# Winograd convolutions: the first output tile of each image takes its products in another order

## The chip, the cores and the metric

The kernel runs on one core of one Trainium2 chip. The metric is the device time of one execution in microseconds. Three runs of the kernel before took 3323.92, 3324.4 and 3329.04 us; the median is 3324.4 us.

## What is computed

The reference is a small image network on three images of 256 channels and 48 x 48 points, in float32, of four residual layers. Layer 0 is a block with attention, layer 3 a state-space scan over the points. The change lies in layers 1 and 2, two 3 x 3 convolutions:

```python
# layer 1: each image has its own kernel, mixed from 8 experts
pooled = x.mean(axis=(2, 3))
routing = sigmoid(pooled @ routing_ws)                    # 3 images x 8 experts
ws = einsum('ne,eoihw->noihw', routing, weight)           # 3 x 256 x 256 x 3 x 3
x = x + conv3x3(gn(x), ws)                                # image n with kernel ws[n]
# layer 2: one kernel and a bias
x = x + conv3x3(gn(x), weight) + bias
```

`gn` is a group norm of 32 groups, which has no learned factors.

## The kernel before, in words

**The convolution.** It is done along image rows in the Winograd form with four outputs and six parts: each group of six neighbouring columns gives six sums (the parts), the three columns of a kernel also give six, and product i of an output tile multiplies part i of the image with part i of the kernel. `products` (L1587) makes one such product: six matmuls of 128 x 128 weights on 128 x 288 values (three kernel rows, two halves of the input channels, `ct` 0 and 1), which add up in one PSUM room `ps_c`. There are five such rooms (pool `ps1`, L1584). The profile counts each of these float32 matmuls twice, so a product is 12 records and an output tile of six products 72.

**The input side.** `input_transform` (L316) works on half an image (24 of 48 rows, `h`). ScalarE first writes the normed values into `xpad` (L331, two instructions), with one row of the other half as a halo, so that it reads x in both halves. Then twelve VectorE steps (L345 to L356) make the six parts `vt`: parts 1 and 3 from two helpers `c` and `e`, parts 4 and 5 from `c` and `e` made anew, last parts 0 and 2 (the outer ones), which use the second `c` and `e`. `xpad` has one buffer, `vt` two. The transform of the next half is made while TensorE multiplies the present one.

**The kernel side.** In the first layer `mixed` (L265) makes the kernel of the next image beside the products of the present one: for each of 8 experts six pieces `wconv` of 128 x 768 come in by DMA (pool `wst`, six buffers), and VectorE adds each, times its routing factor, into `u` (L296). One piece in six is instead added up by TensorE in two spare banks (L282) and copied into `u` by ScalarE at the end (L290). Then `kernel_transform` (L254) turns the three kernel columns, which lie in parts 0, 1 and 2 of `u`, into the six parts, with six VectorE steps for each `ct`: L259 writes part 4, L260 part 5, L262 part 3, L263 part 1. Parts 0 and 2 stay as they came. In the second layer `plain` (L302) loads one kernel for all images.

**The output side.** `output` (L1599) makes one tile: 128 output channels (`m`) of half an image (`h`). It asks for products 1 and 3, then 4 and 5; of each pair ScalarE copies the second out of PSUM (L1607) and VectorE makes the sum and the difference (L1609, L1611). Eight more VectorE steps add these into x, in place (L1616 or L1618, and L1619). At last products 0 and 2 are asked for, and VectorE adds each into x straight from PSUM (L1621, the outer sums).

**The order.** The images go 2, 1, 0, in the first layer and then in the second: six units of two halves of two tiles. The loop over them stands at L1699. For each half the transform of the next half is asked for first, then the two tiles; after each tile 13 steps of the kernel that is being mixed. `moments` (L1628) and `next_norm` (L1648) make the statistics for the next norm on ScalarE. In the second layer the first steps of the scan go in between products (`between`, L1670). The program doesn't fix the order of instructions on an engine here: a scheduler sets it at build time, by what depends on what and its own guess of the costs, and engines then work in that order. Only the part before the convolutions is held in the written order (`keep_order`); in it lies the transform of the first half of image 2 (L1090).

Of the kernel before, what the change touches and what calls it, by code (L numbers as in the profile page):

```python
# [12 lines left out]
ALU = mybir.AluOpType  # L13
# [71 lines left out]
def net(  # L85
# [230 lines left out]
    def input_transform(b, h, sc, sh):  # L316

        rows = HR + 2
        size = rows * PW
        t = pad.tile([P, 4, CT * size + 2], F32, name="xpad")  # L320

        nc.gpsimd.memset(t[:, :, 0 : CT * size + 1 : PW], 0.0)  # L322
        at = (0 if h == 0 else HR + 1) * PW
        for ct in range(CT):
            nc.gpsimd.memset(t[:, :, ct * size + at : ct * size + at + PW], 0.0)
        lo = 1 if h == 0 else 0
        first = h * HR - 1 + lo
        for ct in range(CT):
            src = xs[b][:, ct, :].rearrange("p (j r c) -> p j r c", j=4, c=TW)
            dst = t[:, :, ct * size : (ct + 1) * size].rearrange("p j (r c) -> p j r c", c=PW)  # L330
            nc.scalar.activation(  # L331
                dst[:, :, lo : lo + HR + 1, 1:], src[:, :, first : first + HR + 1, :],
                AF.Identity, bias=sh[:, ct : ct + 1], scale=sc[:, ct : ct + 1],
            )

        def column(j, at):
            return t[:, j, at : at + CT * size].rearrange("p (r c) -> p r c", c=PW)[:, :, :TW]

        d = [column(j, at) for j, at in ((3, 0), (0, 1), (1, 1), (2, 1), (3, 1), (0, 2))]
        vt = vp.tile([P, 6, CT, (HR + 2) * TW], F32, name="vt")  # L340
        o = [vt[:, i].rearrange("p t (r c) -> p (t r) c", c=TW) for i in range(6)]
        c = pad.tile([P, CT * rows, TW], F32, name="wc")
        e = pad.tile([P, CT * rows, TW], F32, name="we")
        tt, stt = nc.vector.tensor_tensor, nc.vector.scalar_tensor_tensor
        stt(c, d[2], -4.0, d[4], ALU.mult, ALU.add)  # L345
        stt(e, d[1], -4.0, d[3], ALU.mult, ALU.add)
        tt(o[1], c, e, ALU.add)
        tt(o[3], c, e, ALU.subtract)
        tt(c, d[4], d[2], ALU.subtract)
        tt(e, d[3], d[1], ALU.subtract)  # L350
        stt(o[4], e, 2.0, c, ALU.mult, ALU.add)
        stt(o[5], e, -2.0, c, ALU.mult, ALU.add)
        tt(o[0], d[0], d[2], ALU.subtract)
        stt(o[0], o[0], 4.0, c, ALU.mult, ALU.add)
        tt(o[2], d[5], d[3], ALU.subtract)
        stt(o[2], e, -4.0, o[2], ALU.mult, ALU.add)  # L356
        return vt

    def routing(b, psum, tag, stats):
# [23 lines left out]
    with ExitStack() as l0:  # L383
# [131 lines left out]
        def hidden(b, c):  # L515
            wf, fb = mlp[b]
            f = fpool.tile([P, 2, CH], F32, name="f")
            pf = pair()
            for m in range(2):
                nc.tensor.matmul(  # L520
                    pf[:, m, :CH], wf[:, m * P : (m + 1) * P], chunk(cur[b], c),
                    start=True, stop=True,
                )
            for m in range(2):
                nc.scalar.activation(f[:, m, :], pf[:, m, :CH], AF.Gelu, bias=fb[:, m : m + 1])
            return f
# [10 lines left out]
        with ExitStack() as p2:  # L537
# [4 lines left out]
            if not exact:  # L542

                sums = vpool.tile([P, 3 * NB * len(SCH) * 16], F32, name="sums")
                nc.gpsimd.memset(sums, 1.0)

            for i in range(NB):
# [399 lines left out]
                vt = vpool.tile([P, NT, 384], F32, name="vt")  # L947
# [27 lines left out]
                if i + 1 < NB:  # L975
# [4 lines left out]
                    for b in ORDER:  # L980
                        for c in range(NCH):
                            f = hidden(b, c)
# [66 lines left out]
        i = NB - 1  # L1049
# [17 lines left out]
        for n, b in enumerate(ORDER):  # L1067
            held = None
            for c in range(NCH):
                f = hidden(b, c)  # L1070
                if held is not None:
                    add_back(i, *held)
                held = b, c, f
                aside(3 if n == 2 and c % 2 else 2)
            add_back(i, *held)
            stats = [
                small.tile([P, NCH, 6], F32, name=f"xst{m}", bufs=2) for m in range(CT)
            ]
            for c in range(NCH):
                concatenated(b, c, *ahead.pop(0))  # L1080

                z = n * NCH + c + 2
                if 3 <= z < len(chunks):
                    ahead.append(parts(*chunks[z]))
                if c:
                    take_stats(b, c - 1, stats)
                if b == 0 and c == 3:
                    vp = late_pool("vp", 2, last_pools)
                    pad = late_pool("pad", stack=last_pools)
                    first_v = input_transform(2, 0, *norms[2])  # L1090
                aside(3 if n < 2 or c < 2 else 99)
            take_stats(b, NCH - 1, stats)
            if b:
                curpools[b].close()
            small_steps.append(routing(b, psm, "m", stats))
# [485 lines left out]
    with ExitStack() as l1:  # L1581
# [5 lines left out]
        def products(u, vt, m, i):  # L1587
            pc = ps.tile([P, 512], F32, tag="c", name="ps_c")
            for ct in range(CT):
                for dy in range(3):  # L1590
                    nc.tensor.matmul(  # L1591
                        pc[:, :HN], u[:, i, dy, ct, m * P : (m + 1) * P],
                        vt[:, i, ct, dy * TW : dy * TW + HN],
                        start=ct == 0 and dy == 0, stop=ct == CT - 1 and dy == 2,
                    )
            between()
            return pc[:, :HN]

        def output(b, h, m, u, vt, bias):  # L1599

            xj = xs[b][:, m, :].rearrange("p (j n) -> p j n", j=4)[:, :, h * HN : (h + 1) * HN]
            tt, stt = nc.vector.tensor_tensor, nc.vector.scalar_tensor_tensor
            sums = []
            for i, j in ((1, 3), (4, 5)):
                pa, pb = products(u, vt, m, i), products(u, vt, m, j)
                cb = tmp.tile([P, HN], F32, name="cb")
                nc.scalar.copy(cb, pb)  # L1607
                add = tmp.tile([P, HN], F32, name=f"add{i}")
                tt(add, pa, cb, ALU.add)  # L1609
                sub = tmp.tile([P, HN], F32, name=f"sub{i}")  # L1610
                tt(sub, pa, cb, ALU.subtract)  # L1611
                sums += [add, sub]
            p, q, r, s = sums
            for k, (minus, more, f) in enumerate(((p, r, 1.0), (q, s, 2.0), (p, r, 4.0), (q, s, 8.0))):
                if bias is None:
                    tt(xj[:, k], xj[:, k], minus, ALU.subtract)  # L1616
                else:
                    stt(xj[:, k], xj[:, k], bias[:, m : m + 1], minus, ALU.add, ALU.subtract)  # L1618
                stt(xj[:, k], more, f, xj[:, k], ALU.mult, ALU.add)  # L1619
            for i, k, f in ((0, 0, 1.5), (2, 3, 6.0)):  # L1620
                stt(xj[:, k], products(u, vt, m, i), f, xj[:, k], ALU.mult, ALU.add)  # L1621


        units = [(layer, b) for layer in range(2) for b in ORDER]
# [38 lines left out]
        def transformed(n):  # L1663
            k, h = halves[n]
            return input_transform(units[k][1], h, *norms[units[k][1]])
# [4 lines left out]
        def between():  # L1670
            next(pending, None)
            if at_unit >= 4:
                next(early, None)
# [23 lines left out]
        vt = first_v  # L1697
        behind, pending = None, iter(())
        for n, (k, h) in enumerate(halves):  # L1699
            layer, b = units[k]  # L1700
            at_unit = k
            if k == 3 and h == 0:
                w3_rooms()
                w3_loads()
            ahead = transformed(n + 1) if n + 1 < len(halves) else None
            u = weights[B if layer else b]
            for m in range(2):
                output(b, h, m, u, vt, v("l2_bias", 0, 2) if layer else None)
                for _ in range(13):
                    next(beside.get(k, iter(())), None)  # L1710
                if m == 0 and behind is not None:
                    store_tokens(*behind)
                    behind = None
            vt = ahead
            if layer:
                behind = b, h
            if h == 1:
                for _ in pending:
                    pass
                pending = next_norm(layer, b)  # L1720
                next(pending)
# [12 lines left out]
    with ExitStack() as l3:  # L1734
# [172 lines left out]
        k = chunks[0]  # L1907
# [7 lines left out]
        for s, (at, m, h) in enumerate(steps):  # L1915
            if m == 0 and h == 1 and at + 2 <= last:
                fetch(at + 2)
            for part in range(8):
                j = 4 * m + 2 * h + part // 4
                scan(s, part)  # L1920
                decay(8 * s + part + 3)
                if (m, h, part) in busy:
                    g, q = parts_of_step[part]
                    keep_busy(tiles[s][:, g, q, 1 : P + 1], busy[m, h, part])
                if part == 0 and h == 0:
                    c, n = (at, m + 1) if m + 1 < DI else (at + 1, 0)
# [31 lines left out]
        k = chunks[last]  # L1958
# [122 lines left out]
```

## Time and profile before

| | |
|---|---|
| median of three runs | 3324.4 us |
| the profiled execution's own time | 3327.43 us |
| its span, first to last instruction | 3325.7 us |
| TensorE busy (matmul) | 3138.1 us, 94% |
| VectorE busy | 2864.1 us, 86% |
| ScalarE busy | 2391.5 us, 72% |
| GpSimd busy | 1334.5 us, 40% |
| convolutions (L1591), first to last matmul | 1499.6 to 1998.0 us |
| matmuls of L1591 | 429.8 us busy, 409 ns mean, x1728 |
| mixing on VectorE (L296) in that stretch | 68.3 us, 1009 ns mean, x70 |

Times inside the profile count from the start of the span. Engines are PE (TensorE's matmuls), PEld (its weight loads, beside the matmuls), DVE (VectorE), ACT (ScalarE), POOL (GpSimd) and SP (which issues DMAs). A row of a timeline gives start, length, engine, line, operation and tiles, and in brackets the idle time of that engine before it and what ended it. A row with xN merges N instructions that follow each other. PEclk is the clock that TensorE was granted, 1.00 being full speed. The convolutions begin after the attention block (which ends at about 1499 us), and the scan follows them.

### The profile page before, as it was taken

How to read it: one execution, taken by the hardware profiler on the slowest of the kernel's cores; microseconds unless marked ns; L12 is line 12 of the kernel's file. 1: busy time of each engine (PE TensorE's matmuls, PEld its weight loads, DVE VectorE, ACT ScalarE, POOL GpSimd, SP SyncE). 2: the span in 40 equal slices, each digit the busy share in tenths (PEclk: the TensorE clock that was granted, in tenths of full speed). 3: DMA queues.
4: the chain of work that ended last, by engine and by line, in shares of the span. 5: the costliest groups of instructions: out<-in, count | busy, mean ns of one | idle time of the engine just before them, and what ended most of it. 6: DMA issues, size and time to landing. Idle time of an engine off the chain costs nothing.

```text
span 3325.7 us, 54145 instructions
## 1 busy us (share of the span) xinstructions
PE 3138.1 (94%) x20890; PEld 1551.0 (47%) x20890; DVE 2864.1 (86%) x3234; ACT 2391.5 (72%) x3663; POOL 1334.5 (40%) x457
## 2 busy tenths in 40 slices
PE   7999999999999999989999997999999999999985
PEld 4334343353343434546677773444444444444442
DVE  3799989968988998379985458999999999999997
ACT  2688888838888887422224457888888888888884
POOL 0000000000000000120000008999999999999997
PEclk9999999999999999999999998999999999999997
DMA  4000000010000001485611025555555555556552
GB/s 167 32 8 10 8 8 7 8 47 5 8 7 8 10 8 32 154 292 186 216 54 42 34 65 138 139 133 126 132 140 147 134 132 132 125 135 144 142 127 56
DMA packets 182158, 290.76 MB, mean 87 GB/s; under 512 B 34737, under 2 KB 148465, under 8 KB 179970
## 3 DMA queue, kind: packets, MB, share of 16 engines
q1 hardware_dynamic: 168658, 267.15, 29.9%
q10 hardware_dynamic: 13232, 20.06, 1.9%
q8 instruction: 165, 2.70, 0.4%
q14 instruction: 103, 0.84, 0.1%
HBM read 236.24 MB, written 50.64 MB: 86 GB/s over the span
## 4 chain that ended last, share of the span: by engine, by line
PE 55%; DVE 30%; ACT 8%; issue 4%; DMA 2%; POOL 0%; SPq 0%; DVEq 0%; ACTq 0%; POOLq 0%
DVE hs L1862 20%; PE ps_s L640 16%; PE acc L653 14%; PE ps_c L1591 8%; DVE hs L1810 3%; ACT ps_da L1854 2%; PE ps_s L1033 2%; PE ps_y L464 2%; PE ps_m L667 2%; PE ps_m L713 1%; DVE u L296 1%; PE acc L531 1%; PE ps_g L1224 1%; PE ps_s L520 1%; PE ps_y L1896 1%
## 5 line engine op out<-in xcount | busy, mean ns | idle before, releaser
L644 ACT ACTIVATE pt<-ps_s 128x1024 f32<-128x1024 f32 x972 | 942.3, 1022 | 154.8 <-PE ps_s L640 142.1
L1862 DVE TENSOR_TENSOR_SCAN hs<-ps_da,hs 128x385 f32<-128x385 f32 x1152 | 1001.9, 934 | 6.8 <-ACT ps_da L1854 4.9
L859 DVE TENSOR_TENSOR part<-part,pt 128x2048 f32<-128x2048 f32 x396 | 906.5, 2289 | 41.3 <-ACT pt L644 18.5
L1854 ACT ACTIVATE ps_da<-dtr,u 128x384 f32<-128x384 f32 x1152 | 651.1, 580 | 119.5 <-DVE hs L1862 108.7
L164 POOL TENSOR_TENSOR rstd<-ve,mhalf 128x2 f32<-128x2 f32 (+1 forms) x26 | 16.7, 642 | 1486.8 <-DVE ve L162 1486.8
L640 PE MATMUL ps_s<-q,kt 32*128 32x512 f32 (+1 forms) x4320 | 576.4, 592 | 0.1
L653 PE MATMUL acc<-pt,vt 128*32 128x512 f32 (+1 forms) x4320 | 521.0, 561 | 0.2
L1591 PE MATMUL ps_c<-vt,u 128*128 128x288 f32 x1728 | 429.8, 409 | 10.8 <-DVE u L263 8.4
L1879 POOL TENSOR_TENSOR hc<-hs,x 128x3072 f32<-128x3072 f32 x72 | 405.2, 5628 | 12.6 <-DVE hs L1862 8.7
L1879 POOL TENSOR_TENSOR hc<-hs,bc 128x3072 f32<-128x3072 f32 x71 | 400.3, 5638 | 9.9 <-DVE hs L1862 5.5
L1591 PEld LDWEIGHTS ps_c<-vt,u 128*128 128x128 f32 x1728 | 328.8, 191 | 106.6 <-DVE u L263 9.1
L640 PEld LDWEIGHTS ps_s<-q,kt 32*128 32x128 f32 x4320 | 195.3, 183 | 199.1 <-issue 120.2
L653 PEld LDWEIGHTS acc<-pt,vt 128*32 128x32 f32 x4320 | 94.4, 108 | 353.4 <-issue 326.7
L1896 PE MATMUL ps_y<-hc,u 128*32 128x384 f32 x2304 | 228.5, 516 | 2.9 <-POOL hc L1879 2.9
L1275 PE MATMUL ps_g<-u 128*128 128x384 f32 x576 | 195.9, 493 | 23.0 <-ACT u L1271 23.0
L1828 POOL TENSOR_TENSOR hs<-dtur,x 128x1536 f32<-128x1536 f32 x72 | 209.0, 2903 | 7.0 <-DMA dtur<-dtud 7.0
L1828 POOL TENSOR_TENSOR hs<-dtur,bc 128x1536 f32<-128x1536 f32 x72 | 209.6, 2912 | 0.0
L1275 PEld LDWEIGHTS ps_g<-u 128*128 128x128 f32 x576 | 108.7, 191 | 107.1 <-ACT u L1271 34.3
L1896 PEld LDWEIGHTS ps_y<-hc,u 128*32 128x32 f32 x2304 | 62.0, 112 | 145.4 <-issue 130.1
L1607 ACT COPY cb<-ps_c 128x288 f32<-128x288 f32 x48 | 19.1, 398 | 152.0 <-PE ps_c L1591 145.0
L322 POOL MEMSET xpad<- 128x212 f32 x12 | 5.7, 472 | 287.4 <-ACT xpad L1642 225.6
L1394 PE MATMUL ps_g<-u 128*128 128x384 f32 x288 | 106.6, 503 | 12.4 <-ACT sz L1402 7.8
(275 smaller groups left out, 4128.8 us busy)
## 6 DMA issues: line engine op xcount, KB each, us to landing
wconv<-in_we SPq DMA_DIRECT2D x144, 384.0 KB, 4.7
dtr<-dtd SPq DMA_DIRECT2D x288, 192.0 KB, 3.7
dtur<-dtud SPq DMA_DIRECT2D x288, 96.0 KB, 4.2
wconv<-xd SPq DMA_DIRECT2D x36, 384.0 KB, 3.7
x<-bcd SPq DMA_DIRECT2D x72, 192.0 KB, 4.7
dtd<-x SPq DMA_DIRECT2D x36, 384.0 KB, 3.0
dtuq<-dtud SPq DMA_DIRECT2D x288, 48.0 KB, 2.0
bc<-bcd SPq DMA_DIRECT2D x72, 192.0 KB, 4.8
```

The lines of the kernel that those rows point to most:

```text
L640: nc.tensor.matmul(s[:, j, cols], kt[r, mt * P : (mt + 1) * P], q[r, :n], start=True, stop=True,)
L644: nc.scalar.activation(p[:, h0 : h0 + 2, :], s, AF.Exp)
L653: nc.tensor.matmul(acc[h * HD : (h + 1) * HD, :n], vt[:, mt, g * P + h * HD : g * P + (h + 1) * HD], p[:, h, cols], start=mt == 0, stop=mt ...
L859: ): nc.vector.tensor_tensor(part, first, p, ALU.add)
L1275: nc.tensor.matmul(bank[m % 2], w3v["taps"][:, m, tap, :], w3v["xi"][:, m % 3, tap : tap + CH], start=tap == 0, stop=tap == DCONV - 1,)
L1394: nc.tensor.matmul(bank[j], w("in", ct * 512 + m * P, P), k.xn[:, ct, DCONV - 1 :], start=ct == 0, stop=ct == CT - 1,)
L1591: nc.tensor.matmul(pc[:, :HN], u[:, i, dy, ct, m * P : (m + 1) * P], vt[:, i, ct, dy * TW : dy * TW + HN], start=ct == 0 and dy == 0, stop ...
L1828: nc.gpsimd.tensor_tensor(states(s)[:, :, 2:4, 1:], chunks[at].rows[m][1].unsqueeze(1).broadcast_to([P, 2, 2, CH]), b_rows(s, 0, 2), ALU.mult,
L1854: nc.scalar.activation(slots[n % 3][:, 1 : CH + 1], chunks[at].rows[m][0][:, q, :], AF.Exp, scale=amat[:, col : col + 1],)
L1862: nc.vector.tensor_tensor_scan(b, slots[(8 * s + part) % 3][:, : CH + 1], b, 0.0, ALU.mult, ALU.add)
L1879: nc.gpsimd.tensor_tensor(hc, tiles[s][:, :, :, 1:], cb.broadcast_to([P, 2, 4, CH]), ALU.mult)
L1896: nc.tensor.matmul(k.y_ps[32 * q : 32 * q + 32, :CH], fold, hc[:, g, q, :], start=False, stop=h == 1 and g == 1,)
```

## The change

In the first tile of each image (h = 0, m = 0) `output` asks for the outer products 0 and 2 first and adds them into x, then for products 4 and 5, then for 1 and 3. The eight steps that add the pairs into x stay as they were, after both pairs. All other tiles keep their order. For h = 0 `input_transform` makes the parts in the order 0, 2, 4, 5, 1, 3: it makes the second `c` and `e` first, and the first `c` and `e`, which parts 1 and 3 need, last. For h = 1 it keeps its order. No instruction is added or taken away, and no size is changed.

```diff
+        def odd():
+            stt(c, d[2], -4.0, d[4], ALU.mult, ALU.add)
+            stt(e, d[1], -4.0, d[3], ALU.mult, ALU.add)
+            tt(o[1], c, e, ALU.add)
+            tt(o[3], c, e, ALU.subtract)
+
+        def outer():
+            tt(o[0], d[0], d[2], ALU.subtract)
+            stt(o[0], o[0], 4.0, c, ALU.mult, ALU.add)
+            tt(o[2], d[5], d[3], ALU.subtract)
+            stt(o[2], e, -4.0, o[2], ALU.mult, ALU.add)
+
         c = pad.tile([P, CT * rows, TW], F32, name="wc")
         e = pad.tile([P, CT * rows, TW], F32, name="we")
         tt, stt = nc.vector.tensor_tensor, nc.vector.scalar_tensor_tensor
-        stt(c, d[2], -4.0, d[4], ALU.mult, ALU.add)
-        stt(e, d[1], -4.0, d[3], ALU.mult, ALU.add)
-        tt(o[1], c, e, ALU.add)
-        tt(o[3], c, e, ALU.subtract)
+        if h:
+            odd()
         tt(c, d[4], d[2], ALU.subtract)
         tt(e, d[3], d[1], ALU.subtract)
+        if not h:
+            outer()
         stt(o[4], e, 2.0, c, ALU.mult, ALU.add)
         stt(o[5], e, -2.0, c, ALU.mult, ALU.add)
-        tt(o[0], d[0], d[2], ALU.subtract)
-        stt(o[0], o[0], 4.0, c, ALU.mult, ALU.add)
-        tt(o[2], d[5], d[3], ALU.subtract)
-        stt(o[2], e, -4.0, o[2], ALU.mult, ALU.add)
+        if h:
+            outer()
+        else:
+            odd()
...
+            def ends():
+                for i, k, f in ((0, 0, 1.5), (2, 3, 6.0)):
+                    stt(xj[:, k], products(u, vt, m, i), f, xj[:, k], ALU.mult, ALU.add)
+
+            first = h == 0 and m == 0
+            if first:
+                ends()
             sums = []
-            for i, j in ((1, 3), (4, 5)):
+            for i, j in ((4, 5), (1, 3)) if first else ((1, 3), (4, 5)):
...
-            p, q, r, s = sums
+            p, q, r, s = sums[2:] + sums[:2] if first else sums
...
-            for i, k, f in ((0, 0, 1.5), (2, 3, 6.0)):
-                stt(xj[:, k], products(u, vt, m, i), f, xj[:, k], ALU.mult, ALU.add)
+            if not first:
+                ends()
```

## The prediction

> **What bounds the kernel now.** First the page's busy rows and chain of waits: TensorE holds the convolutions (its line L1591 is 8% of the chain), VectorE the scan after them. So the question is whether TensorE stands still inside the convolutions, 1499 to 1998 us. The waits of TensorE in that stretch (columns: who waited, for whom, total us, times, longest) answer it:
>
> ```profile
> PE ps_c L1591 <- DVE u L263: 8.4, 2, 6.2
> PE ps_g L282 <- DMA wconv<-in_we: 3.4, 2, 2.2
> PE ps_c L1591 <- DVE u L262: 1.1, 1, 1.1
> ```
>
> Only the kernel transform (L262, L263) costs more than transfers do. The timeline of TensorE says where (start, length, work, idle before it):
>
> ```profile
> 1584.71 2.74 PE L282 MATMUL ps_g<-wconv,each 128*128 128x384 f32 x8
> 1588.00 0.38 PE L186 MATMUL ps_gm<-mv,gmat 128*128 128x2 f32 x2 [0.54 <-ACT xpad L1635]
> 1594.55 20.77 PE L1591 MATMUL ps_c<-vt,u 128*128 128x288 f32 x72 [6.17 <-DVE u L263]
> ...
> 1658.04 17.62 PE L1591 MATMUL ps_c<-vt,u 128*128 128x288 f32 x72
> 1675.50 2.74 PE L282 MATMUL ps_g<-wconv,each 128*128 128x384 f32 x8
> 1680.46 7.54 PE L1591 MATMUL ps_c<-vt,u 128*128 128x288 f32 x30 [2.22 <-DVE u L263]
> 1689.09 22.09 PE L1591 MATMUL ps_c<-vt,u 128*128 128x288 f32 x90 [1.09 <-DVE u L262]
> ```
>
> A tile is 36 matmuls, 72 records. The tile at 1658.04 took 17.62 us, the one after the 6.17 us wait 20.77. The table by stretches of L1591 (busy PE, PEld, then granted clock, DMA share, GB/s) says why:
>
> ```profile
> 1588.00:1591.00 3.00, 0.00 (x0) 0.00 (x0) 0.92 0.95 327
> 1591.00:1594.50 3.50, 0.00 (x0) 0.00 (x0) 0.50 0.09 36
> ...
> 1596.00:1598.00 2.00, 2.00 (x5) 1.36 (x5) 0.50 0.93 356
> ...
> 1600.00:1602.00 2.00, 2.00 (x8) 1.59 (x7) 0.82 0.96 332
> 1602.00:1606.00 4.00, 4.00 (x18) 3.11 (x18) 1.00 0.42 166
> ```
>
> The clock fell to half during the wait and stayed there until about 1601: 20.77 - 17.62 = 3.15 us more. Around the 2.22 us wait at 1680 the same table gives 1.00: no such loss.
>
> **What the Trainium skill says.** "TensorE: Matmul & The Clock Gate", Part 1: TensorE runs at half clock after an idle window of about 3.4 us and recovers after about as long of sustained work. The trace agrees in kind: 0.50 after the 6.17 us wait, 1.00 after 2.22; here the half clock lasted some 6.5 us of work. "Perfetto Trace Analysis", Sequencer Loop: an engine's instructions go into a queue, and one that is read waits there for its semaphores. The trace agrees: the products of parts 0 and 2 had their operands at 1588.8, but stood behind the part that waited until 1594.5. "Trainium Kernel Development and Optimization", Key Constraints: all queues' DMAs run on the same 16 engines; the 0.93 to 0.96 DMA share at 1596 to 1602 agrees.
>
> **The change, part by part.** No instruction is added or removed; the built order differs only within the convolutions, and SP's and POOL's orders not at all.
>
> (a) Image 1's first tile. Before: from the end of the mixing products (1584.71 + 2.74 = 1587.45) to the end of the tile (1594.55 + 20.77 = 1615.3) are 27.9 us, for 17.6 of work: 10.2 lost (idle 6.7, half clock 3.15, and the norm's small product, 0.4, which the built order puts later). After: part 0 of the kernel needs only the last mixing step, which ends before VectorE's first transform step at 1586.48. So the tile starts at 1587.45, each product 17.62 / 6 = 2.9 us. Part 2's second half is wanted at 1591.8 and is there at 1588.8 (ScalarE's L290: 1587.85 + 0.96). From VectorE's timeline: part 4 is there at 1591.9 (L259) and wanted at 1594.7; part 5 at 1593.6 (L260), wanted at 1597.6; part 1, L263, at 1594.5 and 1598.5, wanted at 1599 and 1600.6. No wait is left, so the clock stays up: -10.2 us at the end of this tile, now 1604.9. The image parts were ready (1557.6).
>
> (b) The two outer sums (L1621) now open the tile, and hold two of five PSUM rooms until VectorE adds them into x. They must also wait until ScalarE has read x for the next half (L331, 1591.57 + 2.67 = 1594.2). In the built order they stand on VectorE behind 12 kernel-transform steps and the 11th and 12th of the next half's input-transform steps: the first at 1586.48 + 12 x 0.87 + 11 x 0.72 = 1604.8, done by 1605.3, the second by 1606.4. The first product that needs the room is the next tile's, behind two mixing products (1.3): 1606.2. Cover 0.9 us: I take 0, at worst 1 to 2. Without that cover each us late is a us of TensorE.
>
> (c) Image 1's stage, in which VectorE and DMA mix image 0's kernel:
>
> ```profile
> 1594.50:1680.40 85.90, 83.69 (x322) 62.90 (x322) 79.75 (x133) 17.41 (x27) 1.38 (x4) 0.96 0.64 215
> ```
>
> (Columns: PE, PEld, DVE, ACT, POOL, clock, DMA share, GB/s.) VectorE is busy 79.75 of 85.9 us, so the lead of 10.2 can't all survive. The mixing ended before at 1671.93 (first L258). Up to there VectorE waited some 6.0 us: 4.5 for wconv transfers, 1.1 for a copy, the rest for POOL. The built order now puts 8 steps of the last tile (8 x 0.37 = 3.0) ahead of that end. If no wait shrinks: 1674.9. If all go: 1668.9. I followed TensorE, VectorE and the mixing transfers by hand through the built order (4.7 us from issue to landing, the page's median): VectorE still waits for transfers, TensorE meets four new waits for wconv of 1.6, 1.3, 0.3 and 1.1 us (in-order, all too short to lose the clock), and the mixing ends at about 1671. Its last TensorE product, whose buffer comes free just before, runs to 1672.6 in place of 1678.24. The lead is then 5.6.
>
> (d) Image 0's first tile. Before it ended at 1689.09 + 3.5 x 2.9 = 1699.3, 21.1 after 1678.24: 3.5 lost to waits (2.2 + 1.1). After: part 2 waits for L290, which stands on ScalarE behind the moments (L1635, 2.1 us) of the last tile; about 1673.6, wanted at 1676.5. Part 4 is there at 1676.4, wanted at 1677.9; part 1 at 1683.1, wanted at 1685.1. No wait: 1672.6 + 17.0 (one matmul already done) = 1689.6, so 9.7 ahead. The next tile's first product takes the room of the tile's last and waits for its copy (L1607, 0.4 and the hand-over): +0.6. Left: 9.1. (From the last mixing product to the end of the tile 17.0 us in place of 21.1, so (d) alone gives 4.1.)
>
> (e) Image 2 and the plain convolution. At 1499.67 TensorE is held by ScalarE's L1038, then by VectorE's statistics (1.14 and 0.59): both stay. Part 0 is ready by 1497.5. In the second layer TensorE waited for nothing up to 1855; there the built order puts the outer sums ahead of the transform, so that their rooms are free some 8.5 us into the image, and the earliest user comes at 14.5. 0 +- 0.5.
>
> (f) After the convolutions nothing is changed, and the scan waits for their end through the last store; the lead goes through whole.
>
> Sum: 10.2 (a) - 4.6 (c) + 4.1 - 0.6 (d) = 9.1 us; taken against the profiled execution, 3327.4 - 9.1 = 3318.3. That execution lies 3.0 above the median of the runs, 3324.4; the forecast for the median is 3315.3. Bounds from (c) and (b): mixing at 1674.9 and 1 us of (b) leave 9.1 - 3.9 - 1 = 4.2; mixing at 1668.9 gives 9.1 + 2.1 = 11.2, up to some 12.4 without the new wconv waits.
>
> **Rivals.** Lead eaten: image 1's stage is paced by mixing, and TensorE's earlier start is returned to wconv waits there. For it: VectorE 93% busy, DMA share 0.64. Against: the first-tile waits of image 0 still go. It gives 4.2 to 6.5 us: 3318 to 3320, "same" by the bound below. Mixing keeps up: the transfers, asked for earlier, land earlier, so VectorE's waits go: 3312 to 3313. Slower: the outer sums hold their rooms through the whole next input transform in every image. Price: ScalarE's moments and L331 take until 8 us into an image, the transform another 8.6; rooms are wanted at 14.5, so 2 to 3 us in each of six images, and past some 3.4 us the clock's 3.15 on top; 6 x 3 = 18 takes 9.1 to -9: 3333. It decides once the sums run later than 14.5 us after the image's first product; the built order, which puts them first in the second layer, speaks against it. That the order doesn't change after all is excluded: the built program has part 0 first at all six places.
>
> **How the numbers follow.** A difference under 0.2% (6.6 us) can't be told from no change here. Forecast (6.6 to 11 us gained) 0.62; mixing keeps up 0.13; lead eaten 0.20; slower 0.05. Hence faster 0.75, same 0.20, slower 0.05. The range runs from 3311.0 (12.4 gained, 1 for the runs' scatter) to 3320.5 (4.2 gained).
>
> **What would show it.** TensorE at 1587 without idle and clock 1.00 to 1604 (a); no L1591 wait on the outer sums of more than 1 us (b); waits of L282 for wconv of about 4 us in all, and the last mixing step at 1669 to 1675 (c); image 0's first tile ended near 1690 (d); no new waits after 1700 (e). A wait over 3.4 us anywhere in the stage, with 0.50 behind it, would make the forecast wrong.

## The result, and the profile after

The kernel after takes 3315.88 us (median of 14 runs, 3307.68 to 3322.15) against 3325.24 us before (14 runs, 3322.44 to 3329.51): 9.4 us less, ratio 0.9969 with a 95% interval of 0.996 to 0.9977. (The ratio is an estimate from all runs; that of the two medians alone would be 0.9972.) The forecast was 3315.3 us, a gain of 9.1. The profiled execution took 3316.7 us with a span of 3314.9; the one before took 3327.43, so the two profiles are 10.7 us apart.

In the new file the products stand at L1603 (L1591 before), the outer sums at L1617 (L1621), the copy at L1626 (L1607), `moments` at L1654 (L1635); L258 to L290 are unmoved. TensorE's waits inside the convolutions, without the one before their first product and some on other things of 0.6 us or less (who waited, for whom, total us, times, longest):

```profile
PE ps_g L282 <- DMA wconv<-in_we: 4.4, 4, 2.0
PE ps_gm L186 <- DVE mv L183: 3.0, 1, 3.0
PE ps_c L1603 <- ACT cb L1626: 0.4, 1, 0.4
```

The three waits on the kernel transform (L262, L263), 9.5 us in all, are gone. The timeline of TensorE at the same places, rows left out between them (start, length, work, idle before it):

```profile
1569.05 2.91 PE L282 MATMUL ps_g<-wconv,each 128*128 128x384 f32 x4 [1.96 <-DMA wconv<-in_we]
1584.74 2.74 PE L282 MATMUL ps_g<-wconv,each 128*128 128x384 f32 x8
1587.32 17.62 PE L1603 MATMUL ps_c<-vt,u 128*128 128x288 f32 x72
1669.19 1.53 PE L282 MATMUL ps_g<-wconv,each 128*128 128x384 f32 x4 [0.30 <-DMA wconv<-in_we]
1670.56 17.14 PE L1603 MATMUL ps_c<-vt,u 128*128 128x288 f32 x70
1688.18 19.18 PE L1603 MATMUL ps_c<-vt,u 128*128 128x288 f32 x78 [0.37 <-ACT cb L1626]
1984.08 3.07 PE L1603 MATMUL ps_c<-vt,u 128*128 128x288 f32 x12
```

Image 1's first tile follows the mixing products at once and takes 17.62 us where it took 20.77. Image 0's first tile, but for one matmul done earlier, begins at 1670.56 and is one unbroken row. The last matmul of the convolutions ends at 1987.15, against 1998.44 before: 11.3 us ahead. Of that 0.6 us is lost before the end of the execution. From the timeline before:

```profile
1995.37 3.07 PE L1591 MATMUL ps_c<-vt,u 128*128 128x288 f32 x12
```

The stretches of L1603 that stood at half clock before, now (length of the stretch, busy PE, PEld, then clock, DMA share, GB/s):

```profile
1591.00:1594.50 3.50, 3.50 (x16) 2.77 (x15) 1.00 0.15 61
1596.00:1598.00 2.00, 2.00 (x10) 1.53 (x9) 1.00 1.06 351
1600.00:1602.00 2.00, 2.00 (x10) 1.58 (x9) 1.00 1.02 375
```

Image 1's stage as a whole, in the same view for all engines (length, busy PE, PEld, DVE, ACT, POOL, clock, DMA share, GB/s):

```profile
1587.33:1670.57 83.24, 81.84 (x328) 61.30 (x327) 81.32 (x136) 25.71 (x42) 2.09 (x7) 1.00 0.67 230
```

All that VectorE waits for from 1587 to 1672 us (who, for whom, total us, times, longest):

```profile
DVE u L296 <- DMA wconv<-in_we: 1.5, 3, 0.9
DVE gsc L216 <- POOL rstd L164: 0.4, 1, 0.4
```

VectorE is now busy 81.32 of 83.24 us, 98%; its waits for transfers fell from 4.5 to 1.5 us. TensorE is as busy, 81.84 us, and stood still for 1.4 us only. So neither engine alone limits this stage now; both are full.

### The profile page after: what moved, and what is told of

It reads as the page before. It is cut to its first block, busy times and chain, and to the rows that moved or that the text cites. A ratio compares the mean times of both kernels' runs of the same rounds, so it can differ in the third digit from the quotient of the medians.

```text
span 3314.9 us, 54140 instructions
## 1 busy us (share of the span) xinstructions
PE 3140.8 (95%) x20890; PEld 1553.0 (47%) x20890; DVE 2865.4 (86%) x3234; ACT 2392.1 (72%) x3663; POOL 1335.4 (40%) x457
## 4 chain that ended last, share of the span: by engine, by line
PE 58%; DVE 28%; ACT 7%; issue 4%; DMA 2%; POOL 0%; SPq 0%; DVEq 0%; ACTq 0%; POOLq 0%
DVE hs L1881 20%; PE ps_s L652 16%; PE acc L665 14%; PE ps_c L1603 10%; DVE hs L1829 3%; ACT ps_da L1873 2%; PE ps_s L1045 2%; PE ps_y L476 2%; PE ps_m L679 2%; PE ps_m L725 1%; PE acc L543 1%; PE ps_g L1236 1%; PE ps_s L532 1%; DMA wconv<-in_we 1%; DVE u L296 1%
## 5 line engine op out<-in xcount | busy, mean ns | idle before, releaser
L1603 PE MATMUL ps_c<-vt,u 128*128 128x288 f32 x1728 | 430.6, 409 | 1.7 <-ACT x L1050 1.4
L1603 PEld LDWEIGHTS ps_c<-vt,u 128*128 128x128 f32 x1728 | 329.4, 191 | 98.1 <-issue 3.8
L1626 ACT COPY cb<-ps_c 128x288 f32<-128x288 f32 x48 | 19.3, 402 | 140.1 <-PE ps_c L1603 138.0
```

The lines of the kernel that those rows point to most:

```text
L1603: nc.tensor.matmul(pc[:, :HN], u[:, i, dy, ct, m * P : (m + 1) * P], vt[:, i, ct, dy * TW : dy * TW + HN], start=ct == 0 and dy == 0, stop ...
```

## The experiments

The convolutions begin anywhere from 1494.6 to 1499.8 us in the profiles of eight kernels whose code is the same up to there, and single times scatter by more than that. So beside the time two lengths are read from each trace. Stage 1 goes from the end of the last mixing product of image 1's kernel to that of image 0's; the rest from there to the end of the convolutions. Each length is of one execution: in the four profiles in which image 1's first tile kept the old order and nothing was added ahead of it, stage 1 took 89.3 to 90.8 us, so a difference of some 1.5 us between two rows says little. (The ends of rows overlap the next row by 0.15 us, which is taken off; the expectations quote 411.0 for the 411.1 here.) The times are medians; "ratio" is that to the kernel before on the same chip, whose medians were 3325.1 to 3325.4.

| kernel | time, us | ratio, 95% interval | stage 1 | the rest | sum |
|---|---|---|---|---|---|
| before | 3325.2 | | 90.8 | 320.3 | 411.1 |
| after | 3315.9 | 0.996 to 0.9977 | 83.2 | 316.6 | 399.8 |
| image 1 only | 3323.4 | 0.9986 to 1.0003 | 85.4 | 326.2 | 411.6 |
| image 0 only | 3325.3 | 0.9994 to 1.0011 | 89.3 | 321.1 | 410.5 |
| images 1 and 0 | 3316.8 | 0.9964 to 0.9985 | 83.8 | 316.8 | 400.5 |
| the other four | 3326.7 | 0.9995 to 1.0011 | 90.2 | 319.9 | 410.2 |
| products only | 3319.2 | 0.9971 to 0.9986 | 88.4 | 316.5 | 404.9 |
| kept busy | 3326.0 | 0.9994 to 1.0011 | 87.7 | 321.5 | 409.2 |
| rooms held | 3318.3 | 0.9972 to 0.9985 | 83.1 | 318.3 | 401.4 |
| later routing | 3317.7 | 0.997 to 0.9987 | 84.2 | 316.7 | 400.9 |
| image 0, norm later | 3322.9 | 0.9984 to 0.9997 | 90.2 | 318.5 | 408.7 |
| before, 4 experts | 3316.7 | 0.9966 to 0.9989 | | | 402.3 |
| image 1 only, 4 experts | 3312.1 | 0.9942 to 0.9969 | | | 395.3 |
| after, 4 experts | 3310.3 | 0.9944 to 0.9971 | | | 394.4 |

### One image at a time

Units are numbered in the order of work, so 1 is image 1 and 2 is image 0 of the first layer. `input_transform` gets its new order in the same units. In the first run NEW is (1,).

```diff
-            first = h == 0 and m == 0
+            first = h == 0 and m == 0 and at_unit in NEW
```

> The change for image 1 alone; the other five images keep the old order. Theory (mixing paces image 1's stage, and the two first tiles are worth something only together): TensorE starts image 1's first tile at 1587 without idle, 10.2 us ahead, and reaches image 0's first tile 5 to 7 us ahead. There the old order waits for part 1, which comes only some 2 us earlier, since it hangs on the end of the mixing. So the 2.2 us wait for L263 grows to 7 to 9 us, the clock falls to half, and 3.15 us go on top: the time is within 2 us of before (3323 to 3327). Rival (the gains of the two tiles add up): the 5.6 us that the forecast left of the first tile go through whole, about 3319.6.

Measured: 3323.4 us, 1.7 below before, not to be told from no change. The timeline of TensorE:

```profile
1584.57 17.62 PE L1603 MATMUL ps_c<-vt,u 128*128 128x288 f32 x72
1667.40 2.78 PE L282 MATMUL ps_g<-wconv,each 128*128 128x384 f32 x8
1678.00 33.90 PE L1603 MATMUL ps_c<-vt,u 128*128 128x288 f32 x132 [7.19 <-DVE u L263]
```

L1603 in the stretches of 4 us around its restart (length, busy PE, PEld, clock, DMA share, GB/s):

```profile
1674.00:1678.00 4.00, 0.00 (x1) 0.00 (x1) 0.54 0.55 189
1678.00:1682.00 4.00, 4.00 (x10) 2.82 (x10) 0.61 0.00 0
```

Image 1's first tile is as fast as in the kernel after, and stage 1 is 5.4 us shorter than before. Then TensorE meets the end of the mixing: it waits 7.19 us in place of 2.22 and 1.09, and works at half clock behind that. The rest grows by 5.9 us. The lead is lost whole in this trace, as the theory said.

> The change for image 0 alone. Theory: TensorE arrives at image 0's first tile at the same moment as before, and loses 0 in place of 3.5 us there, less 0.6 for the copy: 3.5 to 4.1 us below before, 3321.1 to 3321.7; no wait for L262 or L263 at that tile, the 6.2 us wait and the half clock at image 1 stay. Rival (the image 0 part is hidden by what comes after): 3325. Rival (most of the whole gain sits here): below 3319.

The same line with NEW = (2,). Measured: 3325.3 us. The gain of 3.5 us did not come, and the theory was wrong. The timeline:

```profile
1670.70 2.74 PE L282 MATMUL ps_g<-wconv,each 128*128 128x384 f32 x8
1673.28 29.26 PE L1603 MATMUL ps_c<-vt,u 128*128 128x288 f32 x120
1702.38 0.28 PE L186 MATMUL ps_gm<-mv,gmat 128*128 128x2 f32 x2
1702.52 4.13 PE L1603 MATMUL ps_c<-vt,u 128*128 128x288 f32 x16
1709.36 0.38 PE L195 MATMUL ps_gv<-gd,gmat 128*128 128x2 f32 x2 [2.71 <-DVE gd L192]
1709.60 67.90 PE L1603 MATMUL ps_c<-vt,u 128*128 128x288 f32 x272
```

The first tile has no wait, as forecast. But 36 us later TensorE stands 2.71 us before the second small product of image 1's norm, which VectorE prepares (L192, at 1709.16), and the clock fell to 0.84 and 0.73 in the two stretches of 4 us from 1708. VectorE, without idle from 1678 on, was still behind with the kernel transform and the sums of image 0, and an earlier TensorE ran into it. The row behind the wait takes 67.90 us; the same 272 records took 66.21 in the kernel before:

```profile
1715.27 66.21 PE L1591 MATMUL ps_c<-vt,u 128*128 128x288 f32 x272
```

So the wait and the slower clock cost 4.4 us, more than the 3.3 us of waits that are gone (2.22 and 1.09).

> The change for image 0 alone once more, with the two small products of image 1's norm put six products later into image 0's stage, behind more of TensorE's work. Theory (the 3.5 us won at image 0's first tile were given back to the wait of 2.7 us on VectorE's part of that norm, and to the slower clock behind it): the wait goes and the gain comes through, from the end of image 2's mixing to the end of the convolutions some 407 us, the time 3 to 4 us below before. Rival (VectorE is late itself, and the wait turns up at the next thing that needs it): 410 to 411 us, the time as before.

```diff
-            for _ in range(9):
+            for _ in range(15 if not layer and b == 1 else 9):
```

Measured: 3322.9 us, 1.0 to 5.3 us below before (from the interval), and 408.7 us in place of 410.5, between the 407 of the theory and the 410 to 411 of the rival. Part of the gain comes through. A wait of 1.47 us is left at the same product, later by 18 us (1727.25). The interval overlaps that of image 0 alone, so that the norm's product took the gain rests above all on the 4.4 us in the trace of image 0 alone; this run bears it out in part.

> The change for images 1 and 0 together; image 2 and the second layer keep the old order. Theory (each of the two is worth nothing without the other): from the end of image 2's mixing products to the end of the convolutions some 400 us as in the changed kernel (399.8), against 411.0 before, 411.6 with image 1 alone and 410.5 with image 0 alone in their profiled runs; the time 9 to 12 us below before, 3313.5 to 3316.5. Rival (the single changes add up, and the rest of the gain comes from the other images): 1.7 + 0, some 3323.5.

NEW = (1, 2). Measured: 3316.8 us and 400.5 us in the trace. The two images alone bring 1.7 and 0 us, both together 8.6; in the traces these are -0.5, 0.6 and 10.6 us. The rival, that they add up, is out.

> The change for image 2 and the three images of the second layer alone, images 1 and 0 in the old order. Theory: no wait there hangs on the order of the parts, 0 +- 1.5 us against before (3325.2). Rival (rooms held by the outer sums): up to 2 to 3 us per image, 3330 or more. Rival (image 2 pays by itself): below 3323.

NEW = (0, 3, 4, 5). Measured: 3326.7 us, ratio 0.9995 to 1.0011, and no new wait in the trace. The other four images do nothing for the time that these runs can show.

### Half of the mixing left out

Image 0's kernel is mixed from four experts in place of eight, in the kernel before, in the kernel after, and in the one with image 1 alone changed. What is left out is half of the additions on VectorE, of the transfers and of the mixing products.

```diff
-        for e in range(EXPERTS):
+        for e in range(4 if b == 0 else EXPERTS):
...
```

> The kernel before, with image 0's kernel mixed from four of the eight experts: half of the mixing that stands beside image 1's stage is left out. Its transform is then ready long before image 0's first tile. Theory: the 3.5 us of waits at image 0's first tile go, four pairs of mixing products (5.2 us) and most of the 3.4 us of wconv waits too; the 6.2 us wait and the half clock at image 1 stay: 3314 to 3317.

> The changed kernel, with image 0's kernel mixed from four of the eight experts, as in the run beside it. Theory (the mixing eats the lead of image 1's first tile): without half of the mixing the lead of 10.2 us goes through whole, 9 to 11 us below the kernel before with four experts. Rival (the lead is lost to something else, or the first tile yields no more than the 5.6 us that were left of it): 4 to 6.5 us below it.

> The change for image 1 alone, with image 0's kernel mixed from four of the eight experts (half of that mixing is left out). With all eight experts this change brought 1.7 us. Theory (there the mixing turned the lead into a wait at image 0's first tile): with half the mixing no wait is left to take it, and the lead of 8 to 10 us goes through: from the end of image 2's mixing products to the end of the convolutions 392 to 395 us, against 402.3 of the kernel before with four experts (394.4 with the whole change); the time 3306 to 3311. Rival (the first tile of image 1 yields little by itself): 400 us or more, 3314 or more.

Measured: 3316.7, 3310.3 and 3312.1 us. The difference of the first two is 6.4 us, short of the 9 to 11 of the theory and within the 4 to 6.5 of its rival; with 10 and 5 runs the two intervals overlap, and the times alone do not decide. The traces give 402.3, 394.4 and 395.3 us, so 7.9 us for the whole change and 7.0 for image 1 alone. Image 1's first tile in this run of before took 19.35 us, not 20.77, so that its wait, half clock and norm product cost 8.8 us there; the 7.9 is most of that. The timeline of image 1 only:

```profile
1587.62 17.62 PE L1603 MATMUL ps_c<-vt,u 128*128 128x288 f32 x72
1651.55 43.92 PE L1603 MATMUL ps_c<-vt,u 128*128 128x288 f32 x180 [1.42 <-DVE sub L1630]
```

Image 0's first tile stands inside the second row, without a wait, where it had waited 7.19 us with all eight experts. There image 1 alone had reached the end with nothing (-0.5 us in the trace). So it is the mixing that takes the lead. Whether its additions or its transfers set the pace these runs don't separate, since both are halved. Nor are the 7.9 and 7.0 us the lead alone: a wait for the norm later on, 1.49 us in this run of before, is 0.25 us with the whole change and none with image 1 alone.

### Single costs

> The kernel before, with the products of parts 0 and 2 made once more ahead of image 1's first tile and thrown away: TensorE works in 5.8 of the 6.7 us in which it stood. Nothing else is changed. Theory of the half clock: the tile takes 17.6 us in place of 20.8, since the clock stays at 1.00, and ends 3.15 us earlier; of that little reaches the end, since the mixing paces the stage: 3323 to 3325.5. Rival (the 3.15 us go through whole): 3322. Rival (the slow start has another cause, such as late operands): the tile still takes 20 us or more.

```diff
+            if at_unit == 1 and h == 0 and m == 0:
+                pc = ps.tile([P, 512], F32, tag="c", name="ps_w")
+                for i in (0, 2):
...
             sums = []
```

Measured: 3326.0 us, no gain. The timeline:

```profile
1597.67 17.73 PE L1591 MATMUL ps_c<-vt,u 128*128 128x288 f32 x72 [1.13 <-DVE u L263]
1681.56 30.87 PE L1591 MATMUL ps_c<-vt,u 128*128 128x288 f32 x120 [3.24 <-DVE u L263]
```

The tile takes 17.73 us: the 3 us were the half clock, and it came from standing still. Stage 1 is 3.1 us shorter than in the profile before (1.6 to 2.5 against the other profiles with the old first tile). Image 0's first tile then has one wait of 3.24 us in place of 2.22 and 1.09, and the clock falls to 0.54 behind it (1681 to 1684), so the rest is 1.2 us longer. Of the 3.1 us 1.9 are left in the trace, and none in the medians, whose interval allows a gain of up to 2 us.

> The changed kernel, but the two outer sums of each first tile are added to x only after the eight steps of the inner sums, so that they hold two of the five PSUM rooms some 4 to 5 us longer. If the rooms are as scarce as the prediction said (cover 0.9 us, beyond it each us late is a us of TensorE): waits of 3 to 4 us of TensorE on the outer sums in image 1's and image 0's second tile, and a time 3 to 8 us above the changed kernel, 3319 to 3324. If the mixing hides it or another room is free: within 1.5 us of it, 3314.5 to 3317.5.

```diff
-            if first:
-                ends()
+            held = {i: products(u, vt, m, i) for i in (0, 2)} if first else None
...
-            if not first:
-                ends()
+            ends(held)
```

Measured: 3318.3 us, 2.4 above the kernel after, between the two expectations, with intervals that just overlap. VectorE adds the outer sums of image 1 at 1608.5 and 1608.9; counted from the start of that image's stage (1585.0 here, 1587.3 in the kernel after) this is 6.0 and 5.3 us later. No wait on an outer sum shows on TensorE; in stage 1 and the next tile it waits 1.1 us for wconv and 0.4 for a copy. So the rooms were not as scarce as the prediction feared; whether the 2.4 us are real stays open.

> The new product order with the input transform of before, which makes parts 0 and 2 last. Only image 2's first half is transformed right ahead of its use, so only there can it matter: its first product waits some 4 us for the image's part 0. Theory (image 2's stage is paced by the mixing of image 1's kernel, so a late start is made up): 0 to 3 us above the changed kernel, 3316 to 3319. Rival (the wait goes through, with half clock behind it): 4 to 7 us above, 3320 to 3323.

Measured: 3319.2 us, 3.3 above the kernel after. TensorE's timeline has this row at the start of image 2:

```profile
1503.93 5.10 PE L1597 MATMUL ps_c<-vt,u 128*128 128x288 f32 x14 [7.50 <-DVE vt L350]
```

The wait is 7.5 us, not 4, in part because the attention block's last product ended 1.9 us earlier than in the profile before, at 1496.4. No loss from it shows further on: from that product to the last mixing product of image 1's kernel are 91.7 us, and in the other profiles this takes 88.6 to 95.4. What is lost lies in stage 1, 88.4 us in place of 83.2, with two waits for wconv of 2.9 and 2.6 us; the scheduler had ordered that stage differently. So the new order of the transform is worth some 3 us in the medians, whose intervals overlap, and 5.1 in the traces, but not by the way that was expected.

> The changed kernel, with the norm and the routing of image 0 begun six products into image 2's stage instead of right at its start (the routing is first wanted in image 1's stage). Theory (the 3.0 us wait of TensorE on these statistics, with the half clock behind it, costs the changed kernel time at image 2): the wait goes, the clock stays at 1.00 at the start of image 2, and the time is 2 to 5 us below the changed kernel, 3311 to 3314. Rival (image 2's stage is paced by the mixing of image 1's kernel, and the wait is hidden by it): within 1.5 us of the changed kernel.

```diff
-            small_steps.append(routing(b, psm, "m", stats))
+            if b:
+                small_steps.append(routing(b, psm, "m", stats))
+            else:
+                stats0 = stats
...
-        behind, pending = None, iter(())
+        behind, pending = None, routing0()
```

Measured: 3317.7 us, within the noise of the kernel after. The edit missed its aim: the wait moved to 1516.59 us, with 2.45 us in place of 3.01, and the clock still fell (0.54 from 1517 to 1520). What that wait costs stays open, and so does whether the mixing hides it: image 2's mixing products end anywhere from 1584 to 1591 us in these profiles.

## Why the prediction was right, step by step

(a) Image 1's first tile: right. It starts at 1587.32 without idle and ends at 1604.94, 10.4 us ahead of before (10.2 forecast). The half clock as cause is shown by the run that was kept busy. Its size is not fixed: behind the same 6.17 us wait the tile took 20.77, 20.44, 19.57, 19.53 and 19.35 us in five profiles, so 1.7 to 3.2 us were lost, and the 3.15 of the forecast's profile was the upper end. Behind the other four its 10.2 would have been 8.8 to 9.9.

(b) The rooms: right for the change. The outer sums ran when the prediction said (1604.8 and 1606.0), and no product waited for them. From VectorE's timeline of the kernel after:

```profile
1604.77 0.45 DVE L1617 SCALAR_TENSOR_TENSOR x<-ps_c,x 128x288 f32<-128x288 f32 x1
1605.85 0.45 DVE L1617 SCALAR_TENSOR_TENSOR x<-ps_c,x 128x288 f32<-128x288 f32 x1
```

The price beyond the cover, "each us late is a us of TensorE", was too high: sums late by 5.3 and 6.0 us made no such wait, and the sum of the two lengths grew by 1.6 us.

(c) The lead eaten in image 1's stage: mechanism right, size off. Forecast was 4.6 us eaten and 5.6 left. The four waits for wconv came to two, 1.1 and 0.3 us in place of 4.3 in sum; the mixing ended at 1670.10 (first L258; about 1671 forecast), its last product on TensorE at 1670.6 in place of 1672.6. So 7.5 us were left. In the profiles with both images changed stage 1 lasts 83.1 to 84.2 us (88.4 with the old transform), in those with neither 90.2 and 90.8 (87.7 where TensorE was kept busy). The mis-sized term is the waits for transfers, those of TensorE above all: 4.3 us forecast, 1.4 measured.

(d) Image 0's first tile: right in the sum, wrong in one sentence. The rest shrank by 3.7 us (3.5 forecast), with the wait for the copy at 0.37 us. But "so (d) alone gives 4.1", read as the gain of this part without the others, fails: alone it gave nothing that the medians show. The step had counted the waits of that tile only and not asked what VectorE, still behind, would owe TensorE next. In the kernel after the same norm step is just in time: VectorE has it ready at 1707.02, and TensorE takes it at 1707.20, without a wait:

```profile
1706.87 0.15 DVE L192 TENSOR_TENSOR gd<-gd,mv 128x2 f32<-128x2 f32 x1
1707.20 0.28 PE L195 MATMUL ps_gv<-gd,gmat 128*128 128x2 f32 x2
```

Here an earlier end of the mixing had helped VectorE too.

(e) The other images: right for the time. "both stay" was loose: the wait for the statistics at image 2 (1.14 us before) lies anywhere from 1.1 to 3.3 us in these profiles, in either order (products only apart, which waited 7.5 us at its start instead).

(f) The lead goes through: 11.3 us at the end of the convolutions, 10.7 in the two profiled times.

So in the profiles the 7.5 of (c) and the 3.7 of (d) give 11.3 (rounded), 2.2 more than the sum of 9.1, and nearly all of that comes from (c). The medians give 9.4 with an interval from 7.6 to 13.3 us. That the forecast median was hit so closely is partly luck. Step (c) left 1.9 us too little of the lead, while step (a) was read from the profile with the dearest half clock of five, by up to 1.4 us. In a usual execution the two errors work against each other.

The rivals: "lead eaten" came true for about 3 of the 10.4 us. With image 1 alone changed, stage 1 is still 5.4 us shorter, and the lead is lost only at image 0's first tile, not to waits for wconv. "Mixing keeps up" is nearer to the profile after (VectorE at 98%, the mixing's end 1.2 us later than its bound of 1668.9). "Slower" didn't occur; in the second layer no wait on the outer sums shows.

## What to carry to other kernels

Two stalls in a row behind one slow engine were worth next to nothing singly here: with the first away, the second grew by about what was won (7.19 us in place of 2.22 and 1.09); with the second away, the next thing that the slow engine owed appeared (2.71 us). Cost such edits together, and for each follow the slow engine's own order one step further than the wait that is removed. Where times scatter by as much as an edit is worth, the length between two fixed points of a trace helps; but it too varied, by some 1.5 us in stage 1, so take it from more than one execution.

## What was not expected of the hardware

The clock fell after shorter waits than the prediction allowed ("past some 3.4 us"), and the length of the wait alone doesn't settle it. Four mixing products take 1.45 to 1.56 us at full clock. From TensorE's timeline of image 1 only:

```profile
1629.81 2.83 PE L282 MATMUL ps_g<-wconv,each 128*128 128x384 f32 x4 [2.29 <-DMA wconv<-in_we]
```

From that of the other four images:

```profile
1571.90 1.56 PE L282 MATMUL ps_g<-wconv,each 128*128 128x384 f32 x4 [3.24 <-DMA wconv<-in_we]
```

After 2.29 us they ran at half clock (as after the 1.96 us at 1569 in the kernel after), and after 3.24 us at full clock. A wait of the same 3.24 us in the run that was kept busy (at 1681.56, above) had a clock of 0.54 behind it. The Trainium skill ("TensorE: Matmul & The Clock Gate", Part 1) speaks of a free-running window of about 3.4 us, and of a penalty that varies from run to run. The loss of 1.7 to 3.2 us behind one and the same wait agrees with that in kind; a fall of the clock after 1.96 and 2.29 us does not follow from a whole idle window, and what decides it was not tried.
